# Three condition networks and the phi products: emitted in the routing stage instead of the end of the expert stage, each held in one large tile

## The chip, the cores and the metric

The kernel runs on one core of one Trainium2 chip. The metric is the device time of one execution in microseconds (us). Everything here is float32 unless noted. TensorE is called PE (its weight loads PEld), VectorE DVE, ScalarE ACT, GpSimd POOL. SyncE, called SP, issues most DMAs; POOL issues the indirect (gather and scatter) ones.

## The reference, cut to what matters

The program is a two-layer network on 32 sequences of 256 tokens with 256 features. In order: a conditioned attention, a conditioned adapter with attention and a mixture of 8 experts, a conditioned linear attention, and a last block whose input is built from several normalised copies of x. The change touches small computations of the two last parts:

```python
def _mlp_ln(s, W1, b1, W2, b2, g, b):                 # the "condition networks"
    h = jax.nn.silu(s @ W1 + b1) @ W2 + b2
    return _ln(h, g, b)
m = x + _mlp_ln(memory_state, mem_W1, ...)[:, None, :]     # memory_state: 32 x 128
n = x + _mlp_ln(noise_state, noi_W1, ...)[:, None, :]      # noise_state: 32 x 64
r = x + _mlp_ln(resource_state, res_W1, ...)[:, None, :]   # resource_state: 32 x 32
...
phi_q = exp(einsum('hmd,bshd->bshm', weights, q)) * scale   # q = x @ Wq.T + bq, likewise k
```

The three networks act on one row per sequence, so each is a matter of a few matmuls with 32 columns. For phi, the kernel multiplies `Wq` and `Wk` by the block-diagonal `weights` once (the "phi products"), so that phi of a sequence is a single projection. All inputs of both are kernel inputs: neither depends on x.

## The kernel before

**Phases.** The first part (up to about 1585 us in the trace) runs the 32 sequences through both attentions and writes two DRAM tables: `h2buf`, the normalised tokens, and `rrows`, the residual. The part that matters here comes after it, in four stages. *Routing*: for each token the two best experts are found and their slots counted, which gives `tok`, the list of tokens by slot (function `routing`, with `choices_of`, `places_of`, `tokens_of`). *Experts*: 8 experts with 4 blocks of 512 slots each, 32 blocks (`expert_block`). *Answers*: for each sequence, the projection `yT` and sums of squares (`answer`, `squares`), then `norms`. *Last block*: `answer_out` for each sequence.

**An expert block** gathers 512 rows of `h2buf` by `tok` (POOL, L1676, four gathers of 128 rows into `xg`), transposes them (PE, L1686, in two halves c=0 and c=1, each copied to `ehT` by ACT, L1689), multiplies with `w1` (`bh`, L1720, eight groups f=0 to 7, ReLU on ACT L1709 or DVE L1707) and `w2` (`by`, L1735), adds the bias and scales by the gate (DVE, L1741 and L1750), and adds the rows to `rrows` with indirect DMAs (POOL, L1643), one after the other, each waiting for the one before. During the experts DVE also folds the butterfly weights of the last block (`butterflies`, the helper `butterfly_stage`).

**Who sets the order.** Each engine executes its instructions strictly in the order in which the program emits them, and that order comes from a planner inside the kernel, `side_by_side`. Every activity is a `Part`: a generator that yields steps such as `yield PE, 0.9` (an engine and an assumed length), waits such as `yield None, 12.0`, and joins with other parts. The planner keeps an assumed free time for each engine and always emits the step that can start first; where two can start at the same time, the one with the lower rank, which is the part's place in the list handed to it. A step that continues on another engine pays an assumed lag of 0.2. Steps called `DVE2`, and steps on POOL, also take a common resource called "port", so they exclude each other in the plan. The plan's lengths are guesses; they decide the order of each engine's queue, nothing else.

**Rings.** Tiles come from rings of fixed size, and a part that asks for a tile when none is left waits, in the plan, until another part gives one back: `mm` (8 PSUM banks), `sh` (20 tiles of 128 x 2 x 256) and `big` (11 tiles of 128 x 8 x 256). Users of `big` at the start of the stage: `w1` and `w2` of two experts (4), the butterflies' `bfb` and `bfw` (2), and in `tokens_of` two tiles `oh`, one for the first and one for the second choices. Each `oh` is written by DVE and ACT, read by the product of L626 on PE, and given back after it.

**The list of parts and the condition networks.** Before, the list begins with `routed, weights_part, loads[0], loads[1], matrices, blocks...`; `loads[e]` issues the weight loads of expert e on SP, `weights_part` five weight matrices of later stages, `matrices` is the butterflies. The networks are started from inside `small_tables` (late: it joins the fourth last expert block), take five `sh` tiles each (the phi products three in all), issue their loads on SP, and then join the last expert block, so that all their computing is emitted behind the last `by` of the experts: L2034 and L2043 (the two matmuls), L2038 (SiLU), L2049 to L2056 (layer norm, with `rsqrt` on POOL, L261 and L267), L2060 (transpose), and for phi L1996, L2001, L2006 and L2008. `small_tables` uses their results in one group of matmuls, L2138. `answer` joins all blocks and all scatters before its first load of `rrows` (L1878), which is followed on PE by L297 (transposes) and L309 (projection).

Of the kernel before, what the change touches and what calls it, by code (L numbers as in the profile page):

```python
# [22 lines left out]
P = 128  # L23
S = 256
D = 256
# [193 lines left out]
def network(ctx: ExitStack, tc: tile.TileContext, a: dict, out: bass.AP):  # L219
    nc = tc.nc  # L220
    T = out.shape[0]
    B = T // S
# [27 lines left out]
    condT = cst.tile([P, B], F, name="condT")  # L250
# [5 lines left out]
    def col(name, c):  # L256
        return cols[:, COL[name] + c : COL[name] + c + 1]

    def rsqrt(o, i, n, eps, op=ALU.add, engine=None):

        (engine or nc.gpsimd).tensor_scalar(o, i, eps, 1.0, op, ALU.mult)  # L261
        power(o, n)
# [66 lines left out]
    def get(r, name, shape=None, dtype=F):  # L329

        pool, own, turns = rings[r]
        yield turns
        return pool.tile(shape or own, dtype, name=name, tag=r)

    def back(r):
        return "back", rings[r][2]
# [1048 lines left out]
    for l in ("k", "o", "c"):  # L1385
        d2 = wA.tile([P, B, 2], F, name="d2_" + l)
        n = B if l == "c" else N0
# [115 lines left out]
    def routing():  # L1503
        yield from choices_of(NT - LATE, NT)
        yield from places_of(NT - LATE, NT)
        counted = Part(ends())
        yield counted
        got = []
        yield from tokens_of(NT - LATE, NT, "big", got)
        both = yield from get("sh", "both", [P, 2, 2, NHI])  # L1510
        to = wD.tile([P, 2, NHI], F, name="to")
        yield "join", counted
        yield DVE, 0.75
        nc.vector.tensor_add(both.rearrange("p k a h -> p k (a h)"), got[0], early)
        yield back("mm")
        yield DVE2, 1.0
        nc.vector.tensor_tensor(to, both[:, 1], late.unsqueeze(1).to_broadcast([P, 2, NHI]), ALU.mult)
        nc.vector.tensor_add(to, to, both[:, 0])
        yield DVE, 0.3
        nc.vector.scalar_tensor_tensor(tok, to[:, 0], float(P), to[:, 1], ALU.mult, ALU.add)  # L1520
        yield back("sh")
        rest.append(Part(gates()))
        yield rest[-1]
        rest.append(Part(slots(to)))
        yield rest[-1]
# [327 lines left out]
    def last_weights():  # L1853
        yield SP, 0.1
        nc.sync.dma_start(ids, a["ids"])
        for t, n in ((cw, "cwT"), (wq["aq"], "aqT"), (wq["ak"], "akT"), (wav, "avT"), (wD_iw2, "iw2")):
            yield SP, 0.1
            nc.sync.dma_start(t, a[n].rearrange("(k p) n -> p k n", p=P))
# [118 lines left out]

    def phi_weights():

        blk = yield from get("sh", "blk", [P, 2, P])  # L1980
        yield SP, 0.1
        nc.sync.dma_start(blk, a["ablk"].rearrange("(k p) m -> p k m", p=P))
        nats = []
        for n in ("aq", "ak"):
            nat = yield from get("sh", "nat")
            nats.append(nat)
            yield SP, 0.1
            nc.sync.dma_start(nat, a[n].rearrange("(k p) i -> p k i", p=P))
        yield None, 2.5
        yield "join", blocks[-1]  # L1990
        for n, nat in zip(("aq", "ak"), nats):
            for i in range(2):
                ps = yield from get("mm", "mm", TS)
                yield PE, 0.9
                for k in range(2):
                    nc.tensor.matmul(  # L1996
                        ps[:, 0, k * P : (k + 1) * P], nat[:, k, i * P : (i + 1) * P], blk[:, k, :],
                        start=True, stop=True,
                    )
                yield DVE, 0.4  # L2000
                nc.vector.tensor_copy(waq[n][:, i, :], ps[:, 0, :])  # L2001
                yield back("mm")
            ps = yield from get("mm", "mm", TS)
            yield PE, 0.4
            for k in range(2):
                nc.tensor.matmul(ps[:, 0, k : k + 1], blk[:, k, :], col(n + "b", k), start=True, stop=True)  # L2006
            yield DVE, 0.2
            nc.vector.tensor_copy(abq[n], ps[:, 0, 0:2])  # L2008
            yield back("mm")
            yield back("sh")  # L2010
        yield back("sh")

    def condition_network(n, src, k, vT):
        ci = condT
        if n != "mem":
            ci = wD.tile([k, B], F, name="ci_" + n)
            yield SP, 0.1
            nc.sync.dma_start(ci, a[src])
        m1 = yield from get("sh", "m1", [k, D])
        m2 = yield from get("sh", "m2")  # L2020
        rb = yield from get("sh", "rb", [B, D])
        yield SP, 0.1
        nc.sync.dma_start(m1, a[n + "W1"])
        yield SP, 0.1
        nc.sync.dma_start(m2, a[n + "W2"].rearrange("(k p) n -> p k n", p=P))
        o, w_ = ROWS_S[n + "b2"]
        yield SP, 0.1
        nc.sync.dma_start(rb, a["rows_s"][:, o : o + w_].to_broadcast([B, w_]))
        yield None, 2.5
        yield "join", blocks[-1]  # L2030
        ps = yield from get("mm", "mm", TS)
        yield PE, 0.4
        for m in range(2):
            nc.tensor.matmul(ps[:, m, :B], m1[:, m * P : (m + 1) * P], ci, start=True, stop=True)  # L2034
        hT = yield from get("sh", "mhT", [P, 2, B])
        yield ACT, 1.8
        for m in range(2):
            nc.scalar.activation(hT[:, m, :], ps[:, m, :B], AF.Silu, bias=col(n + "b1", m))  # L2038
        yield back("mm")
        ps = yield from get("mm", "mm", TS)  # L2040
        yield PE, 0.9
        for c in range(2):
            nc.tensor.matmul(ps[:B, 0, :], hT[:, c, :], m2[:, c, :], start=(c == 0), stop=(c == 1))  # L2043
        u = yield from get("sh", "mu", [B, D])
        st = sm.tile([B, 6], F, name="mst")
        mv = sm.tile([B, 2], F, name="mmv")
        rstd = sm.tile([B, 1], F, name="mrs")
        yield DVE, 1.1
        nc.vector.tensor_add(u, ps[:B, 0, :], rb)  # L2049
        nc.vector.bn_stats(st, u)  # L2050
        nc.vector.bn_aggr(mv, st)
        yield back("mm")
        yield POOL, 0.8
        rsqrt(rstd, mv[:, 1:2], 1, LN_EPS)
        yield DVE, 0.4
        nc.vector.tensor_scalar(u, u, mv[:, 0:1], rstd, ALU.subtract, ALU.mult)  # L2056
        ps = yield from get("mm", "mm", TS)
        yield PE, 0.3
        for c in range(2):
            nc.tensor.transpose(ps[:, c, :B], u[:, c * P : (c + 1) * P], ident[:B, :B])  # L2060
        vT[n] = wD.tile([P, 2, B], F, name="vT_" + n)
        yield DVE, 0.3
        for c in range(2):
            nc.vector.tensor_scalar(
                vT[n][:, c, :], ps[:, c, :B], col(n + "g", c), col(n + "be", c), ALU.mult, ALU.add
            )
        yield back("mm")
        for _ in range(5):
            yield back("sh")

    def small_tables():

# [13 lines left out]
        yield back("sh")  # L2086
        yield POOL, 0.1
        nc.gpsimd.memset(qacc, 0.0)
        vT = {}
        nets = [Part(condition_network(*n, vT)) for n in (("mem", "condT", P), ("noi", "noiT", 64), ("res", "resT", 32))]  # L2090
        for p in nets:
            yield p
        phis = Part(phi_weights())
        yield phis

        awr = wD.tile([P, 6], F, name="awr")
        wsm = wD.tile([P, 6], F, name="wsm")
        ssum = wD.tile([P, 1], F, name="ssum")
# [35 lines left out]
        for m in range(2):  # L2134
            i = 0
# [258 lines left out]
    routed = Part(routing())  # L2394
    loads, blocks = [], []
# [6 lines left out]
    weights_part = Part(last_weights())  # L2402
    matrices = Part(butterflies([]))
    table_part = Part(small_tables())
    first_parts = [Part(answer(b)) for b in range(B)]
    square_part = Part(squares() if NG > 0 else iter(()))
    norm_part = Part(norms([*first_parts, square_part, table_part]))
    with tc.manual_schedule():
        side_by_side(
            [routed, weights_part, *loads[:2], matrices, *blocks, *loads[2:], table_part, *first_parts, square_part, norm_part]  # L2410
            + [Part(answer_out(b, first_parts[-3] if b < 2 else norm_part, [norm_part])) for b in range(B)],
            LAGS_D,
        )
# [125 lines left out]
```

## Time and profile before

| | us |
|---|---|
| median of 3 runs | 3667.69 (3663.62 to 3671.68) |
| the profiled execution | 3662.85, of which the span of the profile 3661.1 |
| PE busy | 3449.3 (94% of the span), matmuls |
| DVE / ACT / POOL busy | 2231.1 / 1791.7 / 1923.0 |
| PE busy, 1550 to 1600 us | 21.35 of 50.00, mean granted clock 0.67 |
| PE busy, 1600 to 1650 us | 36.63 of 50.00, granted clock 0.81 |
| PE busy, 2000 to 2500 us | 500.00 of 500.00, granted clock 1.00 |
| PE busy, 2500 to 2600 us | 93.45 of 100.00, granted clock 0.93 |
| PE busy, 2600 to 2700 us | 100.00 of 100.00 |

A timeline row gives the start, the duration, the engine, the line of the kernel, the operation with its output and inputs, the count of merged instructions, and in brackets how long the engine had been idle before and what ended the idleness. A row of the windows gives a stretch, then for each engine the busy time, then the mean granted clock of PE (1.00 is full speed), the share of time in which the DMA engines moved data, and the GB/s they moved.

The kernel issues these loads for the networks and phi at 2410 to 2469 us, each 0.3 to 0.55 us on SP's queue. The networks' and phi's work on PE lies between 2536.2 and 2557.5 us.

### The profile page before, as it was taken

How to read it: one execution, taken by the hardware profiler on the slowest of the kernel's cores; microseconds unless marked ns; L12 is line 12 of the kernel's file. 1: busy time of each engine (PE TensorE's matmuls, PEld its weight loads, DVE VectorE, ACT ScalarE, POOL GpSimd, SP SyncE). 2: the span in 40 equal slices, each digit the busy share in tenths (PEclk: the TensorE clock that was granted, in tenths of full speed). 3: DMA queues.
4: the chain of work that ended last, by engine and by line, in shares of the span. 5: the costliest groups of instructions: out<-in, count | busy, mean ns of one | idle time of the engine just before them, and what ended most of it. 6: DMA issues, size and time to landing. Idle time of an engine off the chain costs nothing. (4 is left out here: it accounts for less than half of the span.)

```text
span 3661.1 us, 55105 instructions
## 1 busy us (share of the span) xinstructions
PE 3449.3 (94%) x21365; PEld 2520.9 (69%) x21365; DVE 2231.1 (61%) x3614; ACT 1791.7 (49%) x2761; POOL 1923.0 (53%) x1573
## 2 busy tenths in 40 slices
PE   6798999999999999959999999999979999999999
PEld 5465566666666666636666666666968888888888
DVE  7988889888788983656664531011354556555554
ACT  2677787788787877722222222222324343333433
POOL 3645766565566564235546555543044556565553
PEclk9999999999999999979999999999989999999999
DMA  3334344433443442143234333232432322332321
GB/s 88 64 91 101 88 95 103 111 90 94 107 107 89 97 106 57 48 152 89 69 108 102 101 69 66 50 73 35 144 132 63 102 96 95 95 121 89 108 96 44
DMA packets 192239, 332.67 MB, mean 91 GB/s; under 512 B 55041, under 2 KB 116673, under 8 KB 181730
## 3 DMA queue, kind: packets, MB, share of 16 engines
q0 software_dynamic: 56768, 163.68, 20.0%
q1 hardware_dynamic: 135058, 164.86, 14.4%
q8 instruction: 171, 2.80, 0.3%
q14 instruction: 98, 0.80, 0.1%
q10 hardware_dynamic: 144, 0.52, 0.0%
HBM read 204.03 MB, written 52.58 MB: 70 GB/s over the span
## 5 line engine op out<-in xcount | busy, mean ns | idle before, releaser
L1090 ACT ACTIVATE pt<-sc 128x2048 f32<-128x2048 f32 x256 | 481.6, 1881 | 122.0 <-PE sc L1081 115.2
L1709 ACT ACTIVATE hid<-bh,cols 128x512 f32<-128x512 f32 x254 | 173.8, 687 | 618.8 <-PE bh L1720 618.8
L1735 PE MATMUL by<-w,hid 128*128 128x256 f32 x2048 | 454.1, 380 | 2.6 <-DVE ysb L1741 2.6
L1720 PE MATMUL bh<-ehT,w 128*128 128x512 f32 x1024 | 451.3, 594 | 1.0 <-DVE ysb L1741 1.0
L1735 PEld LDWEIGHTS by<-w,hid 128*128 128x128 f32 x2048 | 388.5, 191 | 67.8 <-issue 15.3
L267 POOL TENSOR_TENSOR n<-n,negh 128x32 f32<-128x32 f32 x64 | 366.1, 5721 | 5.3
L1643 POOL DMA_INDIRECT rrows<-ysb,row x128 | 220.2, 1721 | 253.3 <-DMA rrows<-ysb,row 146.8
L1720 PEld LDWEIGHTS bh<-ehT,w 128*128 128x128 f32 x1024 | 195.1, 191 | 220.7 <-issue 214.8
L1741 DVE TENSOR_TENSOR ysb<-by,b 128x512 f32<-128x512 f32 x64 | 44.0, 688 | 469.3 <-PE by L1735 422.1
L1081 PE MATMUL sc<-qT,kT 32*128 32x256 f32 x4096 | 298.3, 406 | 14.2 <-ACT pt L1090 12.5
L1063 PE MATMUL av<-pt,vaug 128*32 128x256 f32 x4096 | 277.9, 390 | 7.2 <-ACT pt L1090 6.4
L893 DVE TENSOR_TENSOR hprod<-hex,kk 128x2048 f32<-128x2048 f32 x120 | 274.9, 2312 | 0.0
L1081 PEld LDWEIGHTS sc<-qT,kT 32*128 32x128 f32 x4096 | 188.0, 187 | 102.4 <-issue 52.5
L2366 PE MATMUL dh<-zT,w_eff 128*128 128x256 f32 x1024 | 235.4, 380 | 0.0
L2380 PE MATMUL do<-w_con,gT 128*128 128x256 f32 x1024 | 233.4, 382 | 0.0
L1676 POOL DMA_INDIRECT xg<-h2buf,tok x128 | 148.0, 1157 | 162.3 <-issue 58.0
L2380 PEld LDWEIGHTS do<-w_con,gT 128*128 128x128 f32 x1024 | 194.4, 192 | 25.5
L2366 PEld LDWEIGHTS dh<-zT,w_eff 128*128 128x128 f32 x1024 | 190.1, 190 | 23.4 <-DVE zT L2342 0.3
L1063 PEld LDWEIGHTS av<-pt,vaug 128*32 128x32 f32 x4096 | 108.0, 110 | 136.3 <-issue 68.6
L261 POOL TENSOR_SCALAR rstd<-mv 128x2 f32<-128x2 f32 x160 | 52.4, 328 | 278.4 <-DVE mv L367 254.4
L261 POOL TENSOR_SCALAR n<-n 128x32 f32<-128x32 f32 x64 | 52.9, 827 | 240.4 <-DVE n L939 239.4
L798 DVE TENSOR_REDUCE hex<-hprod 128x64 f32<-128x1024 f32 (+1 forms) x192 | 166.6, 897 | 1.2
(620 smaller groups left out, 7219.9 us busy)
## 6 DMA issues: line engine op xcount, KB each, us to landing
hprod<-hprod POOLq DMA_DIRECT2D x60, 1024.0 KB, 7.8
oT<-rden SPq DMA_DIRECT2D x64, 256.0 KB
w<-in_w SPq DMA_DIRECT2D x16, 1024.0 KB
x<-rrows SPq DMA_DIRECT2D x64, 256.0 KB
bfw<-in_upw SPq DMA_DIRECT2D x10, 1024.0 KB
bfw<-in_dnw SPq DMA_DIRECT2D x10, 1024.0 KB
xT<-in_xT SPq DMA_DIRECT2D x32, 256.0 KB
avT<-avT SPq DMA_DIRECT2D x256, 32.0 KB
```

Of the source, the lines that this page charges most:

```text
L267: nc.gpsimd.tensor_tensor(o, o, negh[:p].to_broadcast([p, n]), ALU.pow)
L798: nc.vector.tensor_reduce(e[:, t, j0 : j0 + n, :] if exact else e[:, t, 8 : 8 + w // DH, j0 : j0 + n].rearrange("p h j -> p j h"), pr[:, t ...
L893: nc.vector.tensor_tensor(pr.rearrange("p j (h d) -> p j h d", d=DH), weights(t, j0, 8)[:, 0].unsqueeze(3).to_broadcast([P, 8, H, DH]), wi ...
L1063: nc.tensor.matmul(av[32 * i : 32 * i + 32, c % 2, :], va[:, kc, HO * (4 * c + i) : HO * (4 * c + i) + 32], pt[:, i, kc, :], start=(kc == ...
L1081: nc.tensor.matmul(sc[:, i, kc, :], kT[r, m, kc * P : (kc + 1) * P], qT[r, e, m, :], start=True, stop=nm is None,)
L1090: nc.scalar.activation(pt, sc, AF.Exp, scale=1.0 / math.sqrt(DH))
L1643: nc.gpsimd.indirect_dma_start(rrows[:, :], bass.IndirectOffsetOnAxis(ap=row[:, j0 + t : j0 + t + 1], axis=0), y[:, t, :], None, compute_o ...
L1709: nc.scalar.activation(o, ps, AF.Relu, bias=bcol)
L1720: nc.tensor.matmul(ps, w["w1"][:, c, f * P : (f + 1) * P], hT[c], start=(c == 0), stop=(c == 1))
L1735: nc.tensor.matmul(ps[:, t, :], hid[f // 4][:, f % 4, (t0 + t) * P : (t0 + t + 1) * P], w["w2"][:, f, :], start=(f == 0), stop=(f == 7),)
L2366: nc.tensor.matmul(ps[:, g, :], w_eff[:, c, f * P : (f + 1) * P], zT[:, c, :], start=(c == 0), stop=(c == 1))
L2380: nc.tensor.matmul(ps[:, t, :], gT[:, f, t * P : (t + 1) * P], w_con[:, f, :], start=(f == 0), stop=(f == 7))
```

## The change

The networks and phi become parts of their own in the planner's list, right after the first expert's loads, and no longer join the last block. Their tiles are slices of one `big` tile each: three for the networks and one for phi, instead of `sh` tiles. Their wait after issuing the loads becomes 12.0 in the plan instead of 2.5. `weights_part` moves behind the loads of the second expert. The operations, their shapes and their operands are the same.

```diff
     def phi_weights():
-        blk = yield from get("sh", "blk", [P, 2, P])
+        held = yield from get("big", "phi")
+        blk = held[:, 0, :].rearrange("p (k m) -> p k m", k=2)
         yield SP, 0.1
         nc.sync.dma_start(blk, a["ablk"].rearrange("(k p) m -> p k m", p=P))
         nats = []
-        for n in ("aq", "ak"):
-            nat = yield from get("sh", "nat")
+        for i, n in enumerate(("aq", "ak")):
+            nat = held[:, 2 + 2 * i : 4 + 2 * i, :]
...
-        yield None, 2.5
-        yield "join", blocks[-1]
+        yield None, 12.0
...
     def condition_network(n, src, k, vT):
...
-        m1 = yield from get("sh", "m1", [k, D])
-        m2 = yield from get("sh", "m2")
-        rb = yield from get("sh", "rb", [B, D])
+        held = yield from get("big", "net")
+        m1, m2, rb, u = held[:k, 0, :], held[:, 2:4, :], held[:B, 1, :], held[:B, 4, :]
+        hT = held[:, 5, : 2 * B].rearrange("p (c b) -> p c b", c=2)
...
-        yield None, 2.5
-        yield "join", blocks[-1]
+        yield None, 12.0
...
-        for _ in range(5):
-            yield back("sh")
+        yield back("big")
+
+    vT = {}
+    nets = [Part(condition_network(*n, vT)) for n in (("mem", "condT", P), ("noi", "noiT", 64), ("res", "resT", 32))]
+    phis = Part(phi_weights())
 
     def small_tables():
...
-        vT = {}
-        nets = [Part(condition_network(*n, vT)) for n in (("mem", "condT", P), ("noi", "noiT", 64), ("res", "resT", 32))]
-        for p in nets:
-            yield p
-        phis = Part(phi_weights())
-        yield phis
...
-            [routed, weights_part, *loads[:2], matrices, *blocks, *loads[2:], table_part, *first_parts, square_part, norm_part]
+            [routed, loads[0], *nets, phis, loads[1], weights_part, matrices, *blocks, *loads[2:], table_part, *first_parts, square_part, norm_part]
```

More of the change, by code (lines that the diff above doesn't have):

```diff
@@ L2009, in phi_weights @@
             yield back("mm")
-            yield back("sh")
-        yield back("sh")
+        yield back("big")
     def condition_network(n, src, k, vT):
@@ L2034, in condition_network @@
             nc.tensor.matmul(ps[:, m, :B], m1[:, m * P : (m + 1) * P], ci, start=True, stop=True)
-        hT = yield from get("sh", "mhT", [P, 2, B])
         yield ACT, 1.8
@@ L2043, in condition_network @@
             nc.tensor.matmul(ps[:B, 0, :], hT[:, c, :], m2[:, c, :], start=(c == 0), stop=(c == 1))
-        u = yield from get("sh", "mu", [B, D])
         st = sm.tile([B, 6], F, name="mst")
@@ L2067, in condition_network @@
         yield back("mm")
-        for _ in range(5):
-            yield back("sh")
+        yield back("big")
+    vT = {}
+    nets = [Part(condition_network(*n, vT)) for n in (("mem", "condT", P), ("noi", "noiT", 64), ("res", "resT", 32))]
+    phis = Part(phi_weights())
     def small_tables():
```

## The prediction, made before the changed kernel was run

> **What bounds the kernel.** I read the page's first two parts, then windows at the place the work leaves and at the place it goes to, then the timeline of both.
>
> ```profile
> PE 3449.3 (94%) x21365; PEld 2520.9 (69%) x21365; DVE 2231.1 (61%) x3614; ACT 1791.7 (49%) x2761; POOL 1923.0 (53%) x1573
> PE   6798999999999999959999999999979999999999
> ```
>
> PE bounds the kernel except in three dips: slice 18 (about 1550 to 1650 us, the routing), around 2550, and around 2750. Outside them a microsecond of PE work costs a microsecond. The change takes work out of the second dip and puts it into the first, so what counts is what sets the end of each dip. First the one it leaves:
>
> ```profile
> 2522.60 13.98 PE L1735 MATMUL by<-w,hid 128*128 128x256 f32 x64
> 2540.17 1.54 POOL L1643 DMA_INDIRECT rrows<-ysb,row  x1 [3.04 <-DVE mu L2049]
> 2544.67 1.54 POOL L1643 DMA_INDIRECT rrows<-ysb,row  x1 [2.96 <-issue]
> 2548.49 3.42 SPq L1878 DMA_DIRECT2D x<-rrows  x6
> 2551.93 3.65 PE L297 MATMUL mm<-ident,x 128*128 128x128 f32 x16 [2.38 <-DMA x<-rrows]
> 2555.36 0.85 PE L2006 MATMUL mm<-cols,blk 128*128 128x1 f32 x4
> 2556.08 1.09 PE L297 MATMUL mm<-ident,x 128*128 128x128 f32 x4
> 2557.10 0.42 PE L2060 MATMUL mm<-ident,mu 32*128 32x32 f32 x2
> ```
>
> The last expert matmul ends at 2536.58 (2522.60 + 13.98) and the answers' first transpose starts at 2551.93. These 15.35 us belong to the scatters: the last four start at 2531.14, 2535.58, 2540.17 and 2544.67, some 4.5 us apart; then the loads of `x` leave at 2548.49 and land 3.4 us later. The networks and phi sit in that hole, and of their PE work only L2006 and one L2060 come after its end. Now the place it goes to:
>
> ```profile
> 1597.52 3.57 PE L626 MATMUL tps<-oh,ol 128*128 128x256 bf16 x16 [4.01 <-ACT oh L635]
> 1604.78 1.16 POOL L1676 DMA_INDIRECT xg<-h2buf,tok  x1 [23.55 <-DMA bfb<-in_bexp]
> 1615.18 1.33 PE L1686 MATMUL mm<-ident,xg 128*128 128x128 f32 x5 [0.87 <-DMA xg<-h2buf,tok]
> 1615.75 1.57 ACT L1689 ACTIVATE ehT<-mm,cols 128x512 f32<-128x512 f32 x2 [11.42 <-PE mm L1686]
> 1618.18 0.85 PE L1686 MATMUL mm<-ident,xg 128*128 128x128 f32 x2 [0.24 <-DMA xg<-h2buf,tok]
> ```
>
> A chain runs through PE, though PE is mostly idle: the L626 products (first choices, then second) end at 1601.09, DVE makes `tok` by 1603.06, POOL gathers from 1604.78, block 0's fourth gather lands at about 1615.2, `ehT` is done at 1617.32. Then PE still waits for four transposes of block 1, queued ahead of block 0's first `bh`, which starts at 1618.82. From there PE is fed until 2536.58 but for two gaps (2.57 and 0.97 us). So **a delay of this chain goes into the time one for one**.
>
> **What the change takes away.** At the end: L2006 and L2060 leave the path, start to next start 0.72 us (2555.15, its weight load, to 2555.87) and 0.35 us (2557.10 to 2557.45): 1.07. The scatters of 2540.17 and 2544.67 came 4.59 and 4.50 after their predecessors against 4.44 for the undisturbed pair (2531.14 to 2535.58): without DVE and POOL work between, at most 0.2 us, taken as 0.13. The 14 loads on SP before 2469 delayed nobody (PE is at 100.00 of 100.00 from 2400 to 2500). L2138, 24 matmuls and 2.78 us (2562.34 to 2565.12), no longer waits for the networks and moves ahead to about 2480; PE is full at both places: 0.
>
> *The row against a rule.* The 1.07 us run in the slow stretch:
>
> ```profile
> 2550.00:2555.00 5.00, 3.07 (x15) 3.00 (x16) 1.03 (x4) 1.68 (x4) 1.17 (x10) 0.50 0.87 302
> 2555.00:2560.00 5.00, 5.00 (x19) 4.16 (x18) 0.69 (x3) 2.40 (x6) 0.00 (x0) 0.50 0.01 2
> 2560.00:2565.00 5.00, 5.00 (x34) 4.59 (x33) 2.84 (x6) 0.00 (x0) 0.10 (x1) 0.94 0.15 56
> ```
>
> The third column from the right is the granted clock: 0.50 until about 2560. The Trainium skill ("TensorE: Matmul & The Clock Gate", Part 1) says that the clock rises after a stretch of *time* under load (about 3.4 us), not after a number of matmuls. By the rows' durations I save 1.07. By the rule the slow stretch ends when it ended before, and the work drawn forward into it would otherwise have run at full speed: the gain is half, 0.54. The rows agree in kind (slow for 8 us of nearly continuous work, longer than the rule's figure), so I take 0.54. The rule also warns that emptying the hole lets the clock drop; the rows show that it had dropped anyway. **Gain 0.54 + 0.13 = 0.67 us**, between 0.3 and 1.3.
>
> **What it adds at the front: the order.** The order comes from the plan, so I walked through its assumed times by hand (used for order only). Of 11 `big` tiles these are taken at once: four of the experts, one each for mem, phi and `bfb`; then noi, res and `bfw`: ten. `tokens_of` gets the eleventh for the first `oh`, and **the second `oh` must wait until the first product gives its tile back**: planned 11.3, so the second product is ready at 14.7 (before: 12.1). Meanwhile SP has planned the loads by 0.8 (mem), 1.2, 1.6 and 1.9 (phi); plus 12.0 and the lag, PE takes L2034 of mem at 13.0, noi at 13.4, res at 13.8 and phi's L1996 at 14.2. All four stand on PE's queue **ahead of the second routing product**, which follows at 15.1. Each waits for its own loads, and the routing waits behind them.
>
> **When those loads land.** The trace does not show it. Ahead of and including `nat<-in_aq` stand expert 0 (1.05 + 1.05 + 0.13 MB), the networks (0.43 + 0.37 + 0.33) and phi's first two (0.13 + 0.26): 3.75 MB from an issue at 1588.9.
>
> ```profile
> 1590.00:1595.00 5.00, 1.31 (x20) 0.98 (x20) 3.61 (x19) 0.00 (x0) 0.00 (x0) 0.50 0.74 236
> 1595.00:1600.00 5.00, 2.48 (x12) 1.69 (x13) 4.86 (x13) 2.30 (x2) 0.00 (x0) 0.50 1.00 327
> 1600.00:1605.00 5.00, 1.09 (x6) 0.43 (x3) 3.80 (x13) 0.63 (x1) 0.22 (x1) 0.84 0.93 346
> ```
>
> The last column gives 1.26 MB by 1595, 2.90 by 1600 and 4.63 by 1605 (5 us times GB/s, with 0.08 before), so 3.75 MB by 1602.5. SP is not later: 16 issues of some 0.5 us end near 1597. I take **1602.8**. Lower bound 1599.3, where the products' own order rules; upper bound 1608.6, if the second expert's 2.23 MB behind it share the engines evenly (5.98 MB on the same rates, with 375 GB/s after 1605). I take the value near the low side because the first `bfw` fits transfers in order: 8.0 MB of SP's loads and 1.4 MB of gathers by its landing at 1618.0, and the rates sum to 9.5.
>
> **The sum of the chain.** Then phi's four matmuls (1.22 us on a slow clock, the row at 2547.97) and the second product (half of 3.57: 1.79) end at 1605.8, against 1601.09: +4.7. `tok`, the gathers and their landing move by as much: 1615.2 becomes 1619.9. The transposes and `ehT` took 1615.18 to 1617.32, so 1622.0. What block 0 no longer waits for is block 1: on POOL the plan has block 0's gathers to 22.8, then the networks' three `rsqrt` (0.8 each, with a `DVE2` step of 0.7 among them), then block 1's gathers at 25.93, and so block 1's transposes at 35.33, behind block 0's first `bh` at 35.30, whose lower rank then keeps all eight `bh` ahead. Without that wait `bh` starts at 1622.0 against 1618.82: **+3.2**. Block 1's four transposes (0.13 each warm: 1.04 for 8) and the gate's transpose (0.14), which lay in the idle stretch, now take PE's time: +0.65. **Cost 3.85 us.**
>
> **Moved, at nothing.** The other PE work (L2043, L2060, the rest of L1996, L2006) follows the second product and ends before block 0's fourth gather or within 0.5 us of it; cover: the gathers' 10.4 us. POOL's three `rsqrt` pairs (0.93 each: 2547.22 less 2546.29, so 2.8) stand between block 0's and block 1's gathers; cover: eight `bh`, 15 us; price without it 2.8. DVE's 7.5 us (three times 1.9 and the phi copies, 1.8) go before the gates, which end 1617 now and are needed near 1645; likewise SiLU's table load of 1.28 and the one back to Exp. The butterflies' first weights come behind 1.5 MB more, 4.6 us later; DVE has until 2560. The four `big` tiles are back before `hid` asks.
>
> **Forecast**: 3.85 - 0.67 = +3.2. The profiled execution, 3662.85, becomes 3666.0. The median of the runs lies 4.8 above that execution, so the forecast is 3667.69 + 3.2 = **3670.9**: no difference worth the name. About 0.2% (7.3 us) is what a measurement of this kernel can tell from no change.
>
> **Rivals.** (a) *Block 1 stays ahead of `bh`.* The planned margin is 0.03, so one misread step turns it. Then the first `bh` waits for POOL: 4.7 + 2.8 = 7.5, less 0.67: 3674.5. Against it: only my walk through the plan. (b) *The loads land late*: PE stands before phi's L1996 and holds the routing. Each microsecond beyond 1602.8 costs one; from 1606.9 the result is slower beyond the bound. At 1608.6 it is 3.2 + 5.8 = 9.0: **3676.7, slower**. For it: a DMA share of 1.00 in that stretch, and 512-byte rows in `blk`. Against it: the `bfw` sum above. (c) *The hold does not bite*: loads by 1599.3, then only the `oh` tile delays, 1.5 us, covered by the vanished wait for block 1; and the two PE gaps of 2.57 and 0.97, waits for DVE, close as the butterflies shift: 0.65 - 0.67 - 3.5 = -3.5: 3664.2. Nothing in the trace offers more than 7 us of gain, as the hole at 2537 to 2552 stays with the scatters.
>
> **Chances**: forecast 0.45 (own range 3667 to 3675), (a) 0.2, (b) 0.2, (c) 0.15. A shifted plan can rearrange the later stages by a few us either way, so beyond 3675.0 I put 0.05 of the forecast, 0.1 of (a), all of (b): 0.35; below 3660.4 0.05 of (c) and 0.05 of the forecast: 0.10. Range 3661 to 3681.
>
> **What would show it.** Right: PE idle ahead of L1996 near 1599 to 1603 on DMA, L626 in two groups with phi between, the first `bh` near 1622 with block 1's transposes behind it, PE empty from the last `by` to the answers, L297 then at the same distance from the last scatter. Wrong: L626 in one group, `bh` before 1619 or past 1625, a shorter hole at the end, or new PE gaps in the experts.

## The result and the profile after

The changed kernel took 3679.67 us (median of 6 runs, 3674.5 to 3682.1), the kernel before 3663.63 us on the same chip (6 runs, 3658.19 to 3671.68): a ratio of 1.0047, 95% interval 1.0036 to 1.0059. It is slower by 16 us, five times what the likeliest case said. The profiled execution took 3677.17 us, its span 3675.4.

From here on a profile is cut at four marks: the first step of the last phase's routing on DVE (L548), block 0's first `bh`, the end of the last `by`, and the answers' first transpose (L297). What runs ahead of the first mark is the same program in every kernel here, and still ended anywhere between 1579.9 and 1593.4 us from one profiled execution to another; so stages are compared, and single spans are not.

| us | front, L548 to `bh` | experts, to the end of `by` | to the answers' L297 | the rest |
|---|---|---|---|---|
| before | 29.94 | 917.76 | 15.35 | 1109.17 |
| after | 36.52 | 935.71 | 14.38 | 1106.43 |
| difference | +6.58 | +17.95 | -0.97 | -2.74 |

The four differences sum to +20.8, where the medians differ by 16.0: each row is one profiled execution, and the part ahead of the first mark was 6.5 us shorter in that of after. So a stage is known to a few us, not to tenths.

The first two parts of the page of after, the lines that answer to those shown of before:

```profile
PE 3446.3 (94%) x21365; PEld 2517.9 (69%) x21365; DVE 2227.2 (61%) x3614; ACT 1793.7 (49%) x2761; POOL 1931.1 (53%) x1573
PE   6799999999999999869998999998979999999999
```

PE has as much work as before (3446.3 against 3449.3 us), yet of the 40 slices (92 us each) two that were nines are eights now: the 22nd, 1930 to 2021 us, in the middle of the experts, and the 28th, 2481 to 2573, the hole at the end, which the networks had partly filled. In the windows by stage of each kernel (stretch, then PE, PEld, DVE, ACT and POOL busy, granted clock, DMA share, GB/s) the experts are the second row of either; here they stand alone, before first:

```profile
1618.82:2536.58 917.76, 914.22 (x3336) 613.25 (x3335) 355.12 (x495) 224.94 (x338) 495.63 (x376) 1.00 0.33 77
```
```profile
1618.88:2554.59 935.71, 920.80 (x3361) 617.74 (x3361) 361.31 (x512) 225.13 (x338) 509.08 (x379) 0.99 0.32 74
```

PE stood idle for 3.5 us before and 14.9 after: 11.4 of the 17.95. Another 6.6 are in the busy time: 2.8 are L2130 (the table of the networks' columns, L2138 before), which moved into this stretch and is missing from the rest (-2.74); most of the other 3.8 is PE running slowly after the holes (e5 below has the same instructions and no hole, and PE is busy for 914.66 us, 6.1 less than here). The timeline of after, at the two holes and at what lies ahead of the first:

```profile
1839.75 1.63 POOL L1676 DMA_INDIRECT xg<-h2buf,tok  x1 [18.61 <-DVE bfb L1779]
...
1866.10 3.08 DVE L1777 TENSOR_TENSOR bft<-w_eff,bfw 128x512 f32<-128x512 f32 x3 [9.97 <-DMA rrows<-ysb,row]
...
1874.64 0.68 DVE L1779 TENSOR_TENSOR bfb<-bft 1x512 f32<-1x512 f32 x1
...
1875.59 1.64 POOL L1676 DMA_INDIRECT xg<-h2buf,tok  x1 [6.94 <-DVE bfb L1779]
...
1944.69 1.79 POOL L1676 DMA_INDIRECT xg<-h2buf,tok  x1 [0.30 <-issue]
...
1950.17 0.95 POOL L1676 DMA_INDIRECT xg<-h2buf,tok  x1 [0.30 <-issue]
...
1955.53 0.48 PE L1686 MATMUL mm<-ident,xg 128*128 128x128 f32 x1 [4.97 <-DMA xg<-h2buf,tok]
1957.18 0.48 PE L1686 MATMUL mm<-ident,xg 128*128 128x128 f32 x1 [1.18 <-DMA xg<-h2buf,tok]
...
1983.89 3.06 DVE L1777 TENSOR_TENSOR bft<-bfx,bfw 128x512 f32<-128x512 f32 x3 [10.09 <-DMA rrows<-ysb,row]
...
1994.63 0.68 DVE L1741 TENSOR_TENSOR ysb<-by,b 128x512 f32<-128x512 f32 x1
...
1995.37 1.97 PE L1686 MATMUL mm<-ident,xg 128*128 128x128 f32 x8 [8.76 <-DVE ysb L1741]
```

Read the second hole first. PE's bracket says 8.76 us, ended by DVE's `ysb`. Go up to DVE: it did not come to `ysb` before 1994.63, since it works in order and had stood 10.09 us in front of `bft`, one of the three products of a butterfly step, which has nothing to do with PE's work here. What ended that wait is a scatter (`rrows<-ysb`): the slot of the `sh` ring that `bft` was given had held a `ysb` which the scatter was still reading.

In the first hole PE waits for the gathers that left at 1944.69 to 1950.17. POOL, which issues them, worked without a pause from 1927.25 on; its queue was late from further back. The gathers' tiles `xg` take slots of the same `sh` ring, and at 1839.75 and 1875.59 POOL had stood 18.61 and 6.94 us in front of a gather until DVE's butterfly step had read its `bft` (L1779). Ahead of the second of these DVE itself had stood 9.97 us for a scatter. So the ring couples both ways: DVE waits for POOL's scatters, and POOL's gathers, with later scatters behind them, wait for DVE.

At the front, the timeline of after:

```profile
1590.99 1.86 PE L626 MATMUL tps<-oh,ol 128*128 128x256 bf16 x8 [4.00 <-ACT oh L635]
...
1594.48 1.03 PE L2032 MATMUL mm<-ci_noi,net 64*128 64x32 f32 x4 [0.94 <-DMA net<-in_noiW]
...
1595.02 0.47 SPq L1989 DMA_DIRECT2D phi<-in_aq  x1
...
1598.68 1.19 PE L1996 MATMUL mm<-phi 128*128 128x128 f32 x4 [2.14 <-DMA phi<-in_aq]
1599.67 1.92 PE L626 MATMUL tps<-oh,ol 128*128 128x256 bf16 x8
...
1605.27 1.16 POOL L1676 DMA_INDIRECT xg<-h2buf,tok  x1 [30.52 <-DMA w<-in_w]
...
1616.20 0.85 PE L2006 MATMUL mm<-cols,phi 128*128 128x1 f32 x4
...
1616.91 1.95 PE L1686 MATMUL mm<-ident,xg 128*128 128x128 f32 x8
...
1618.88 9.32 PE L1720 MATMUL bh<-ehT,w 128*128 128x512 f32 x17
```

Two groups of L626, the networks and phi's first product between them, PE idle on phi's load, and eight transposes of block 0 alone ahead of `bh`: the order that the prediction walked through. And the hole that the work left:

```profile
2540.61 13.98 PE L1735 MATMUL by<-w,hid 128*128 128x256 f32 x64
...
2562.46 1.55 POOL L1643 DMA_INDIRECT rrows<-ysb,row  x1 [2.95 <-issue]
2566.37 3.77 SPq L1878 DMA_DIRECT2D x<-rrows  x6
2568.97 1.97 PE L297 MATMUL mm<-ident,x 128*128 128x128 f32 x8 [14.38 <-DMA x<-rrows]
```

It is empty of PE work now and still 14.38 us long: the scatters own it.

### The profile page after: what moved, and what is told of

Its sections match the earlier page's. It is cut to its first block, busy times and chain, and to the rows that moved or that the text cites. A ratio compares the mean times of both kernels' runs of the same rounds, so it can differ in the third digit from the quotient of the medians.

```text
span 3675.4 us, 55099 instructions
## 1 busy us (share of the span) xinstructions
PE 3446.3 (94%) x21365; PEld 2517.9 (69%) x21365; DVE 2227.2 (61%) x3614; ACT 1793.7 (49%) x2761; POOL 1931.1 (53%) x1573
## 5 line engine op out<-in xcount | busy, mean ns | idle before, releaser
L1081 PE MATMUL sc<-qT,kT 32*128 32x256 f32 x4096 | 296.8, 404 | 14.5 <-ACT pt L1090 12.7
L1633 POOL DMA_INDIRECT gslot<-gbuf,grow x128 | 148.5, 1160 | 43.0 <-issue 38.4
```

Of the source, the lines that this page charges most:

```text
L1081: nc.tensor.matmul(sc[:, i, kc, :], kT[r, m, kc * P : (kc + 1) * P], qT[r, e, m, :], start=True, stop=nm is None,)
```

## The experiments

Two questions: is the longer experts stage a matter of the plan or of the moved work, and what in it makes PE wait? And what holds the front? All times are against the kernel before in the same session (its median 3661.68 us in the first four, 3659.75 in the next four, 3658.28 in the last four); stages are from one profile of each, which can lie some us from the median (e9's execution took 3651.50 us, e12's 3667.83); "holes" are PE's waits over 0.3 us in the experts.

| kernel | time, us | ratio, 95% interval | front | experts | holes |
|---|---|---|---|---|---|
| e1 | 3681.09 | 1.0050 (1.0031 to 1.0068) | 45.06 | 921.73 | 4.3 |
| e2 | 3668.66 | 1.0022 (1.0012 to 1.0032) | 28.53 | 938.22 | 15.4 |
| e3 | 3670.97 | 1.0025 (1.0016 to 1.0034) | 28.78 | 928.97 | 13.2 |
| e4 | 3678.87 | 1.0041 (1.0024 to 1.0058) | 33.52 | 932.60 | 12.5 |
| e5 | 3660.81 | 1.0007 (0.9998 to 1.0015) | 38.08 | 914.66 | none |
| e6 | 3658.00 | 0.9996 (0.9985 to 1.0007) | 30.65 | 917.22 | 2.2 |
| e7 | 3682.99 | 1.0055 (1.0040 to 1.0069) | 42.09 | 936.77 | 15.8 |
| e8 | 3675.37 | 1.0042 (1.0030 to 1.0054) | 37.54 | 929.10 | 11.7 |
| e9 | 3641.81 | 0.9948 (0.9929 to 0.9967) | 27.67 | 912.10 | none |
| e10 | 3656.31 | 0.9986 (0.9973 to 0.9998) | 34.73 | 914.51 | none |
| e11 | 3664.37 | 1.0011 (0.9998 to 1.0024) | 34.01 | 928.00 | 8.7 |
| e12 | 3655.18 | 0.9986 (0.9977 to 0.9996) | 29.13 | 919.94 | 5.9 |

**e1: the work moved, the plan of the experts as before.** The networks' and phi's steps get the length 0 in the plan and tiles outside the `big` ring, and `weights_part` stands in its old place:

```diff
-            [routed, loads[0], *nets, phis, loads[1], weights_part, matrices,
+            [routed, weights_part, loads[0], *nets, phis, loads[1], matrices,
...
-                yield PE, 0.9
+                yield PE, 0.0
```

> The networks and phi run in the routing stage as in the change, but their steps have length 0 in the plan, their tiles are their own, and the list keeps its old places for the other parts, so that every other instruction of the experts stands in the order of the kernel before (POOL's order differs in 2 rows). Theory A (the loss is the changed order of the expert stage): the two PE holes of 6 and 9 us near 1950 to 1995 are gone, the experts take 918 to 922 us as before, and the time is that of before plus 0 to 4 us (ratio 1.000 to 1.0012). Theory B (the loss is the moved work and its loads themselves, held on PE and POOL during routing): the time stays that of the changed kernel, ratio 1.004 to 1.005.

The experts came back to 921.73. The front did not do as expected: 45.06. With lengths of 0 the three `rsqrt` stand on POOL ahead of block 0's gathers, so the first gather left at 1620.99, 31.6 us after the first routing step, against 15.9 before. That also ate the time that was expected to come back: the ratio is 1.0050, not 1.000 to 1.0012.

**e2: the plan of the changed kernel, no work moved.** Parts without instructions take the networks' and phi's turns in the plan; the real ones run late, as before, but with the length 0 in the plan and in tiles outside the rings:

```diff
+    def network_ghost(n):
+        yield rings["big"][2]
...
+        yield PE, 0.4
+        yield ACT, 1.8
...
-            [routed, loads[0], *nets, phis, loads[1], weights_part, matrices,
+            [routed, loads[0], *ghosts, loads[1], weights_part, matrices,
```

> The reverse: the changed kernel's plan to the row (parts that take the same steps and turns in the plan, but emit no instruction, stand where the networks stood), while the networks and phi run behind the last expert block as before. Theory A: the holes are there again and the time is 10 to 15 us above before (ratio 1.0027 to 1.004), some less than the changed kernel because PE and POOL are not held by loads in the routing stage. Theory B: the time of before, ratio 0.9995 to 1.0005.

Experts of 938.22 with the two holes of after (5.74 and 8.17 us) in the same places, and a front of 28.53. With e1 this is a two by two. The experts follow the plan (918 and 922 against 936 and 938). The front is long where the work was moved (29.9 and 28.5 against 36.5 and 45.1), though e1's also has another order on POOL. So the loss in the experts is no cost of the moved work at all. In time e2 loses less than was expected, 0.22% (0.27 to 0.40% was expected; the changed kernel loses 0.47%), as its front is 1.4 us and its rest 4 us shorter than before. The shorter rest is no merit of the plan: with length 0 all PE work of the networks and phi, and the 24 matmuls of the table (L2138 before), fell into the hole ahead of L297, where PE is idle anyway (an estimate: 2.8 for the table, 1.07 for L2006 and L2060, from the profile of before).

**e3: the list alone.** The kernel before, only `weights_part` behind the first two loads:

```diff
-            [routed, weights_part, *loads[:2], matrices,
+            [routed, *loads[:2], weights_part, matrices,
```

> The kernel before with one edit: weights_part stands behind the loads of the second expert in the list. Theory A (any shift in the plan can open or close holes in the experts): the order of the experts changes (POOL 478 rows moved), so the expert stage may differ from 918 us by several us either way. Theory B: no work is moved, so the time is that of before within 0.05%.

Experts of 928.97 with other holes (1.32 and 1.60 for gathers, 10.29 at `bh`). A harmless looking shift in the list is enough to open them.

**e4: the changed kernel without the `big` tiles.**

```diff
-        held = yield from get("big", "net")
+        held = {"mem": wcat[:, 0:4, :], "noi": wcat[:, 4:8, :], "res": res_own}[n]
```

> The changed kernel with tiles of their own for the networks and phi, so that nothing of the big ring is taken: the second oh tile no longer waits for the first product in the plan, and the second routing product stands ahead of the networks on PE. Theory A: yet another order of the experts (POOL 612 rows moved against before), so the expert stage is not that of either kernel; the routing stage is 3 us shorter than in the changed kernel (36.5 us from its first DVE step to the first bh), as PE no longer holds the second product for the loads. Theory B: only the 3 us of the routing stage are gained, the experts still take 936 us, ratio near 1.004.

The front fell by 3.0 us, and the two routing products run as one group again. What is left of the front's loss sits elsewhere. The timeline of e4 (L2057 is L2056 of the changed kernel):

```profile
1605.89 1.16 POOL L1676 DMA_INDIRECT xg<-h2buf,tok  x1 [23.40 <-DMA w_con<-in_aq]
...
1616.64 0.95 POOL L1676 DMA_INDIRECT xg<-h2buf,tok  x1 [0.30 <-issue]
1617.66 0.18 POOL L261 TENSOR_SCALAR mrs<-mmv 32x1 f32<-32x1 f32 x1
...
1619.04 0.41 PE L2057 MATMUL mm<-ident,res_own 32*128 32x32 f32 x2 [3.65 <-DVE res_own L2053]
...
1620.40 1.06 PE L1686 MATMUL mm<-ident,xg 128*128 128x128 f32 x4
```

The gathers start 15.9 us after the first routing step, as early as before. But the third network's `rsqrt` stands on POOL behind block 1's gathers, PE waits for it in front of L2057, and block 0's transposes wait behind that until 1620.40.

**e5: the butterflies' products in tiles of their own.** The changed kernel; the turn in the `sh` ring is still taken and given back, so the order on every engine is the same, and only what DVE waits for differs:

```diff
-            r = yield from get("sh", "bft", [p, FF // 2])
-            t.append(r.rearrange("p (nb s) -> p nb s", s=s))
+            yield from get("sh", "bft", [p, FF // 2])
+            t.append(bft_own.tile([p, FF // 2], F, name="bft", tag="bft").rearrange("p (nb s) -> p nb s", s=s))
```

> The changed kernel with the three products of each butterfly step (tag bft) in a small pool of their own; the order of every engine's instructions is that of the changed kernel, only VectorE's waits differ. Theory A (VectorE stands in front of a product whose slot is still read by a scatter, and so hands ysb to TensorE late): the hole of 8.76 us before L1686 near 1995 goes, with the slow TensorE clock behind it; the experts fall from 935.7 to 924-928 us, the time from 3679.7 to 3669-3672. The hole before 1955-1957 (gathers) stays. Theory B (the denser plan makes TensorE wait for something anyway): another hole of the same size takes its place, the time stays within 3 us of 3679.

More than was expected: both holes are gone, the experts take 914.66 us, and in them PE is busy without a break:

```profile
1620.61:2535.27 914.66, 914.66 (x3361) 614.05 (x3361) 360.62 (x512) 225.08 (x338) 506.58 (x379) 1.00 0.34 76
```

The gathers' hole had been expected to stay. The timeline of e5 shows why it went:

```profile
1925.53 0.99 POOL L1676 DMA_INDIRECT xg<-h2buf,tok  x1 [0.30 <-issue]
...
1929.33 0.95 POOL L1676 DMA_INDIRECT xg<-h2buf,tok  x1 [0.30 <-issue]
...
1950.60 1.04 PE L1686 MATMUL mm<-ident,xg 128*128 128x128 f32 x8
```

These are the same four gathers (the 14th group of four on POOL's queue, whose order is the same in both): they leave at 1925.53 to 1929.33 instead of 1944.69 to 1950.17, and the transposes at 1950.60 find them landed. POOL's waits for L1779 in front of gathers, 25.5 us in after, are gone. The expectation had taken the second hole for DVE's and the first for the traffic's; both came from `bft` in the `sh` ring. A larger ring with `bft` still in it was not tried.

**e6: the same tiles in the kernel before.** Same edit.

> The kernel before with the same three tiles of their own, same order on every engine. Theory A: the same wait costs the kernel before little, because its plan put the scatters elsewhere: at most the hole of 2.57 us near 1837 goes with its slow restart, time 3657-3663 against 3663.6. If it falls by more than 8 us the wait was a burden of both plans and not what the change brought. Theory B: within 1 us of before.

0.9996 (0.9985 to 1.0007): nothing. This is the other half of the explanation, because the kernel before had the same wait. Its list of DVE's waits in the experts (line waited at, releaser: us in all, times, longest), and then that of after:

```profile
DVE bft L1777 <- DMA rrows<-ysb,row: 60.3, 10, 16.2
...
DVE ysb L1741 <- DMA rrows<-ysb,row: 10.2, 1, 10.2
```
```profile
DVE ysb L1741 <- DMA rrows<-ysb,row: 48.1, 4, 22.2
DVE bft L1777 <- DMA rrows<-ysb,row: 47.4, 8, 10.1
```

In before DVE waited 60.3 us for scatters in front of `bft`, and PE lost 3.5 us to it at most (its two waits for `ysb`, 2.57 and 0.97). In after the sum is smaller there (47.4), but 48.1 us of waits stand in front of `ysb` itself, against 10.2. So the amount of waiting in front of `bft` doesn't tell the cost; what stands behind the waiting instruction does.

**e7: the networks' and phi's loads on ACT's queue.**

```diff
-        nc.sync.dma_start(nat, a[n].rearrange("(k p) i -> p k i", p=P))
+        nc.scalar.dma_start(nat, a[n].rearrange("(k p) i -> p k i", p=P))
```

> The changed kernel with the loads of the networks and of phi issued by ScalarE instead of SyncE, all orders otherwise the same. Theory A (the loads land late because SyncE's issues follow one another, 12.7 us for the list): phi's first product starts 3-4 us earlier against the first routing step (16.3 us now, 12-13.5 then), the front falls from 36.5 to 32.5-34, the time by 3 us. Theory B (the transfers themselves are slow while many small rows move): phi's product within 1 us of 16.3 us, front and time the same within 1.5 us.

A miss for both theories: the front grew to 42.09. The timeline of e7 (ACTq is ACT's queue):

```profile
1588.27 0.60 ACTq L2024 DMA_DIRECT2D net<-in_noiW  x1
...
1595.59 0.33 ACTq L2027 DMA_DIRECT2D net<-in_rows_s  x1
...
1599.42 1.15 ACT L635 ACTIVATE oh<-o,prow 128x1024 bf16<-128x1024 bf16 x1 [19.52 <-issue]
1600.62 1.86 PE L626 MATMUL tps<-oh,ol 128*128 128x256 bf16 x8 [12.79 <-DMA w<-in_w]
```

ACT issued in order and stood 6.7 us before its seventh load. The profile doesn't name what it waited for there; in after the same load waited on SP's queue for a weight of 1 MB (the list in the next section). Behind the issues stood ACT's one-hot L635 for the first routing product, which now left at 1599.42. Whether SP's issue time or the transfers set the landing, e7 doesn't tell.

**e8: the transposed butterfly stages read one set of weights.** The changed kernel; nine of ten loads `in_dnw` are left out, and the stages after the first use its weights:

```diff
-            nc.sync.dma_start(
-                w.rearrange("p k i j -> p (k i j)"), a["dnw"][st : st + 1, :].to_broadcast([P, 2 * FF])
-            )
+            if st == NST - 1:
+                w = wD.tile([P, FF // 2, 2, 2], F, name="bfw_once")
+                nc.sync.dma_start(w.rearrange("p k i j -> p (k i j)"), a["dnw"][st : st + 1, :].to_broadcast([P, 2 * FF]))
```

> The changed kernel where the ten transposed butterfly stages all use the weights of the first of them, loaded once: nine loads of 1 MB left out, the order otherwise the same. Theory A (the gathers xg land late because such a load and the next expert's two weights leave with them): the holes of 4.97 and 1.18 us before 1955-1957 go or fall under 1.5 us together, experts shorter by 5-9 us, time 3670-3675. The hole of 8.76 near 1995 stays (its cause is VectorE's wait). Theory B (POOL issued the gathers too late for TensorE whatever the traffic): the first holes stay within 1.5 us of 6.15, time within 3 us of 3679.

The gathers' holes fell from 6.15 to 0.93 us, the other one stayed (10.75), the experts fell by 6.6. So the first hole needed both: gathers that left late, and a burst of loads to meet them. Taking away either removes it, or nearly so.

**e9: e2 with the butterflies' tiles of e5.** The products get slices of one fixed tile, in which the late networks also sit afterwards:

```diff
-            r = yield from get("sh", "bft", [p, FF // 2])
-            t.append(r.rearrange("p (nb s) -> p nb s", s=s))
+            yield from get("sh", "bft", [p, FF // 2])
+            t.append(bfts[:p, 2 * i : 2 * i + 2, :].rearrange("p a b -> p (a b)").rearrange("p (nb s) -> p nb s", s=s))
```

> The kernel of e2 (the changed kernel's plan, the networks and phi done late as before, nothing of them in the front) with the butterflies' products in tiles of their own. Theory A (the longer experts stage was VectorE's wait for scatters all along, whatever the work moved): the experts fall from 938.2 in e2 to 914-920 us without a hole over 3 us on TensorE, the front stays 28-29, the time falls from 3668.7 to 3646-3653, which is under the kernel before. Theory B (the plan itself packs the experts worse): experts above 928, time above 3660.

3641.81 us, 0.9948 (0.9929 to 0.9967): faster than both kernels, and below what was expected. The new plan is not worse once `bft` has left the ring: against e2 the experts fell by 26.1 us. That it is better than the old plan by all of the 0.52% is not shown. Against before the stages up to L297 are 8.5 us shorter; the rest is 7.2 shorter (1101.96 against 1109.17), of which some 4 is the work that fell into the hole as in e2, and the other 3 are as much as lies between two profiles of one program (1105.34 in e5, 1102.15 in e10, whose instructions on PE are the same there). PE fills all of the experts:

```profile
1620.95:2533.05 912.10, 912.10 (x3340) 612.09 (x3340) 354.71 (x496) 226.44 (x339) 510.24 (x380) 1.00 0.35 78
```

**e10: e5 with phi's first product behind the second routing product.** The first product's matmuls and copy are issued with the second's, one step later; loads and all other orders stay:

```diff
+                todo = [] if (n, i) == ("aq", 0) else [(0, ps0), (1, ps)] if n == "aq" else [(i, ps)]
+                ps0 = ps
```

> e5 with the first of phi's products put behind the routing's second product on TensorE, every other order the same. Theory A (the front is long because TensorE stands at phi's product until its load lands, with the routing's second product behind it): the second L626 starts 2.5-3.5 us earlier against the first routing step (18.5 us in e5), the front falls from 38.1 to 34.5-36 us, the time from 3660.8 to 3657-3659. Theory B (the front is set behind it, by the networks' chain ahead of block 0's transposes): the second L626 is early, the front stays within 1 us of 38.

The second group of L626 starts 14.85 us after the first routing step (1597.55 less 1582.70) instead of 18.53, and the front falls by 3.35 to 34.73: theory A.

**e11 and e12: the butterflies' tiles in e4 and in e3.** The edit is that of e5; in e11 the third network also moves from a tile of its own into the one that phi uses.

> e4 (the networks and phi in the front, in tiles outside the big ring, so with another plan) with the butterflies' products in tiles of their own. Theory A: e4's holes (6.70 us at L1811 behind bfb, 5.80 at bh) came from the same wait: experts from 932.6 to 914-921, front 33.5 as in e4, time from 3678.9 to 3660-3665. Theory B: they have another cause and stay, time above 3670.

> e3 (the kernel before with only weights_part behind two of the loads, no work moved) with the butterflies' products in tiles of their own. Theory A: experts from 929.0 to 914-919, front 28.8 as in e3, time from 3671.0 to 3652-3658, under the kernel before. Theory B: experts above 925, time above 3664.

e11: the time is in the expected range and e4's two holes are gone, but the experts fell only to 928.00, against 914 to 921 expected, and of the holes that are left (8.7 us) 7.5 are waits for gathers: POOL had waited 4.68 us for one scatter after another ahead of them, and DVE still stood 34.0 us in front of `ysb` for scatters. e12: the time is as expected and under the kernel before (0.9986), though its experts (919.94) are a little above the 914 to 919 expected, and its profile, the slowest of its executions, still has two holes of gathers (3.65 and 2.20). So `bft` in the `sh` ring is the largest source of holes, not the only one; what holds the gathers in e11 and e12 is open, as no run here removed it.

## Why the prediction was right in its order and wrong in its sum

The range (3661 to 3681) held the time. The likeliest case did not: +3.2 us was forecast and +16 came, beyond its own range (3667 to 3675). That the range held is luck. Its upper end came from loads that land late (rival (b), 3676.7) and a few us for a shifted plan, not from what cost the time; and the forecast started from 3667.69, while the kernel before then ran at 3663.63: 16 us on the first would have been 3683.7, outside.

**The order on PE, POOL and in front of `bh`: right**, as the rows of the front show. Rival (a) is out, since no transpose of block 1 comes before `bh`. The price of the transposes that then take PE's time stood in the sum.

**The end, a gain of 0.67 us: not measured.** Only its 0.13 for the scatters lies in the hole, which was 0.97 shorter. But e2, e6 and e9, with the networks at the end as before, have 14.88, 14.60 and 14.77 us there against 15.35 in the one profile of before, so profiles differ by more than the term. The other 0.54 lies behind L297's start, in the rest, which differs by 3 us between e5 and e10; so the choice between 0.54 (the rule on the clock) and 1.07 (the rows' durations) stays open. That moving L2138 is worth 0 fits: +2.8 in the experts, -2.74 in the rest.

**The front, +3.2 forecast and +6.58 measured: a right mechanism with one term too small.** The term is "When those loads land": 1602.8, that is 13.9 us after the first routing step. Phi's product started 16.3 after it (1598.68 less 1582.36), and the second routing product ended 19.2 after it, not 16.9. The sentence that carried the term was "SP is not later: 16 issues of some 0.5 us end near 1597", 8.1 us after that step. The load of `in_aq` was issued 12.7 us after it. Some issues took 1.2 us and more, and four of them had to wait, by after's list of waits on SP's queue (line, releaser: us in all, times, longest):

```profile
SPq L2027 <- DMA w<-in_w: 1.2, 1, 1.2
SPq L2024 <- DMA net<-in_memW: 0.9, 1, 0.9
SPq L2022 <- DMA net<-in_memW: 0.5, 1, 0.5
SPq L2017 <- DMA b<-in_b: 0.4, 1, 0.4
```

In all four the name fits the load eight issues ahead on the queue; in the first it is one of the expert's two weights of 1 MB. e10 confirms what stands behind the term: with phi's product out of the way the front loses 3.35 us. The other 1.1 is the cover claimed for the rest of PE's work ("ends before block 0's fourth gather or within 0.5 us of it"): L2006 ended at 1617.05, while the transposes it held could have begun earlier; in e2 the fourth transpose began 6.3 us after its gather's issue, which here would be 1615.5. e4 shows the same chain through POOL's `rsqrt` with a larger price.

**The experts, "a few us either way" forecast and +17.95 measured: the step that failed.** (2.8 of it are L2138.) The prediction priced DVE's moved work and the butterflies' later weights by DVE's deadline ("DVE has until 2560") and concluded that they cost nothing; rival (c) even had PE's two gaps close. What it left out is that DVE works in order, and that butterfly steps sit between the `ysb` that PE's buffers wait for, in slots that a scatter may still be reading and that POOL's gathers wait for in turn. Idle time of DVE was taken for slack. Its list of waits in before, with 60.3 us in front of `bft`, was there to be read: a wait that costs nothing only as long as the plan leaves nothing due behind it. e2 shows that this loss needs none of the moved work, e5 that it goes when `bft` leaves the ring (ratio 1.0047 to 1.0007; experts 935.71 to 914.66), e6 that the old plan lost nothing to it.

What is left in e5 against e9 (1.0007 against 0.9948, some 21 us) holds the price of the moved work itself: a front of 38.08 against 27.67 us, for about nothing at the end. The other half is not broken down. Done as it is, the move doesn't pay. The list of what would prove the forecast wrong did name "new PE gaps in the experts", and those are what came; "`bh` past 1625", 36.1 us after the first routing step, was just met too, with 36.52.

## What to carry to other kernels

An idle engine that works in order has no slack at the instruction it waits in front of: ask what is queued behind it, and who waits for that. A ring of buffers shared by a fast user (`bft`), a slow reader (a chain of scatters, some 4 to 4.5 us apart) and the gathers couples them wherever a plan happens to bring them together, so before the price of a reordering is put at "a few us", list the waits of the engines that are not the bottleneck and give such pairs separate buffers. And when a change shifts a plan, test the plan without the work, and the work without the plan: here that split in two runs what one timing had mixed.

## What the runs showed of the hardware

PE comes back slowly after a hole. Windows of after, behind the hole that ended at 1995.37 (third column from the right: granted clock):

```profile
1990.00:1995.00 5.00, 0.00 (x0) 0.00 (x0) 4.93 (x7) 0.00 (x0) 4.39 (x3) 0.61 0.58 206
1995.00:2000.00 5.00, 4.63 (x15) 4.09 (x16) 4.93 (x8) 1.55 (x2) 0.50 (x1) 0.50 0.23 28
2000.00:2005.00 5.00, 5.00 (x21) 4.25 (x21) 4.93 (x6) 0.00 (x0) 3.96 (x3) 0.87 0.19 55
```

The clock falls within the idle 8.76 us and stands at 0.50 until 2000 and at 0.87 on average until 2005, so a hole costs more than its length. The Trainium skill ("TensorE: Matmul & The Clock Gate", Part 1) has the same behaviour with a shorter climb of about 3.4 us; here it is about 6 us (a mean of 0.87 over 2000 to 2005 is 0.50 until 2001.3 and 1.00 from there, counted from 1995.37).

An engine that issues DMAs is not free meanwhile: in e7 fourteen small loads kept ACT from 1583.68 to 1599.4, 6.7 us of it between two of them.
